# Turning the convolution's result back into rows: 32 by 32 squares on VectorE with a trip through DRAM in place of TensorE transposes

## The chip, the cores and the metric

The kernel runs on one core of a Trainium2 chip. The metric is the device time in microseconds (us) of one execution. Times inside an execution come from one profiled execution, counted from its first instruction. The engines are called PE (TensorE), DVE (VectorE), ACT (ScalarE), POOL (GpSimd) and SP (SyncE, which here only issues DMAs). Weight loads of PE are listed apart as PEld, the issue of a DMA as SPq or ACTq.

## What is computed

One layer on `x` of shape (8, 256, 512): a mixing step and a mixture-of-experts step, each behind a layer norm and with a residual.

```python
x = x + xattn(layernorm(x), k, bias, ctx, ctx, num_heads=8)
x = x + ffn(layernorm(x), gate_w, shared_*, exp_*)

# xattn: D = 256 is split in H = 32 heads of 8 rows, L = 512
kv  = v[:, :, :, None, :] * ctx[:, :, None, :, :]        # 8 x 8 products per head
y   = causal_convolution(kv, k) + kv * bias              # along L, one kernel k per head
out = einsum("bhijl,bhil->bhjl", y, ctx)                 # summed over i
# ffn: shared = silu(x wg) * (x wu) @ wd, plus the top 2 of 8 experts by sigmoid scores
```

The second layer norm needs whole rows: for a row (batch, d), all 512 positions l.

## The kernel before

**Tiles and layouts.** There are 16 tiles of 128 rows (8 batches by 16 values of d); a tile t holds heads 2t and 2t+1. Outside the convolution, a tile is "rows": 128 rows on the partitions, 512 l in each. The convolution wants l on the partitions: four blocks of 128 l, each with 128 rows. Its products with Toeplitz matrices of `k` (L402) run on PE; POOL makes `kv` (`make_kv`, L362); DVE weighs the PSUM result with `ctx` and sums over i into `convT` (`weigh`, L464 and L473), still with l on the partitions. From head 10 on (`H9`) a head takes nine block products in place of ten, with an extra product `same` (L433) and DVE additions (L461).

**Two ways to turn a tile that are there already.** Rows are turned for the convolution and for the shared expert as 32 by 32 squares: ACT writes the normed rows to DRAM (`xv_d` L320, `xn_d` L329), SP reads them back as four quarter loads (`quarters`, L290) so that each 32-row band sits in its place, and one DVE transpose of 128x512 turns all squares (`squares_T`, L296). The last tile, and the first two, go through PE instead: four transposes with the identity into PSUM (L274).

**The result's way back.** `add_skip` (L526) adds the skip term to `convT` of tile t-1 in even head 2t. At the end of that head, behind its convolution products and steps of the shared expert, `residual_T` (L531 to L535) puts four PE transposes into a PSUM tile. In odd head 2t+1, `add_residual` (L538) adds it to the rows of `x2`; bn_stats (L236), ACT's square root, reciprocal and scale follow, then `second_norm` (L326) writes the normed tile to `xn_d`, and SP reads it back as quarters.

**The order of the work is written out by hand.** The loop over 32 heads (L892) emits every engine's instructions in program order, and each engine, and SP's queue, runs its own in that order:

```python
load_toeplitz(h + 2)                 # SP
if not odd: load_tile(t + 3); load_residual(t - 1)   # SP: x1, ctxT, x2
if h == 3: load_shared()             # SP: 4.3 MB of shared weights
...
pss = conv_products(h)               # PE
...                                  # odd: quarters of v, add_residual(t - 1), quarters of f
...                                  # even: add_skip(t - 1), square_vT(t + 1), square_xfT(t - 2)
make_kv(h + 2)                       # POOL
while done < h - 9 + h // (H - 1) and steps[done][0] <= h:
    settle(); step()                 # PE: one step of the shared expert, from head 10 on
if not odd and t > 0:
    residual_T(t - 1)                # PE
```

In heads 0 to 9 the second `weigh` of a head stands behind these DVE operations and the first ahead of them; from head 10 on both stand behind. PSUM for the convolution and the shared expert is one pool of three tiles of two banks (`ps_acc`); an early head takes two of them, so head h+1 needs what `weigh` of head h read first. The transposes' PSUM tiles are the pool `ps_tp` (two tiles). [...] After the heads come the last steps of the shared expert and then the routed experts in blocks of 128 rows, which gather rows from `xn_d` (L1029).

The order of l inside a row (`_orders`, `_laid_out`, L1200 to L1261) is chosen on the host: inputs and weights come permuted, and the result is permuted back.

Of the kernel before, what the change touches and what calls it, by code (L numbers as in the profile page):

```python
# [8 lines left out]
F32 = mybir.dt.float32  # L9
I32 = mybir.dt.int32  # L10
AF = mybir.ActivationFunctionType
ALU = mybir.AluOpType
# [3 lines left out]
P = 128  # L16
B, D, L = 8, 256, 512
NH = 8
H = D // NH
NT = 16  # L20
R = D // NT
NTOK = NT * P
NLB = L // P
# [17 lines left out]
Q = 32  # L41
NQ = P // Q
# [23 lines left out]
def tile_xattn_moe(  # L66
# [29 lines left out]
    V, G, A, T, S = nc.vector, nc.gpsimd, nc.scalar, nc.tensor, nc.sync  # L96
# [3 lines left out]
    def pool(name, bufs=1, stack=ctx, **kw):  # L100
        return stack.enter_context(tc.tile_pool(name=name, bufs=bufs, **kw))
# [4 lines left out]
    dram = pool("dram", space=bass.MemoryType.DRAM)  # L106
    rows = pool("rows", 4)
# [7 lines left out]
    x1, x2, ctxT, tzs = {}, {}, {}, {}  # L115

    def load_tile(t):
        if t < NT:
            x1[t] = cvp.tile([P, L], F32, tag="x1", name=f"x1_{t}")
            S.dma_start(out=x1[t], in_=xv[t])  # L120

            ctxT[t] = cvp.tile([P, NLB + 2, B, R], F32, tag="ctx", name=f"ctxT_{t}", bufs=CTXBUFS)
            S.dma_start(out=ctxT[t], in_=cT[t])
# [6 lines left out]
    def load_toeplitz(h):  # L130

        if h < H:
            tzs[h] = cvp.tile([P, NTZ], F32, tag="tz", name=f"tz_{h}", bufs=TZBUFS)
            S.dma_start(out=tzs[h], in_=toep[h])
# [23 lines left out]
    for e in range(NEXP):  # L158
# [6 lines left out]
        out=upper,  # L165
        in_=upper,
# [30 lines left out]

    xn_d = dram.tile([NTOK + P, L], F32, name="xn_d")
    xv_d = [dram.tile([P, L], F32, name=f"xv_d{t}") for t in range(NT)]
    NCOL = NEXP * CPE  # L200
    table = dram.tile([P * NCOL, 2], F32, name="table")
    zero = rows.tile([P, L], F32, tag="xg", name="zero")
    G.memset(zero, 0.0)
    S.dma_start(out=table.rearrange("(p c) f -> p (c f)", p=P), in_=zero[:, : 2 * NCOL])
    S.dma_start(out=xn_d[NTOK:, :], in_=zero)
# [71 lines left out]
    vT, convT, xfT, xn1, xn2 = {}, {}, {}, {}, {}  # L277
# [31 lines left out]
    def first_root(t):  # L309
        mean, var = ahead[t]  # L310
        ahead[t] = mean, root(f"1_{t}", var, 1.0 / L)
# [213 lines left out]
    def add_skip(t):  # L525
        V.tensor_tensor(convT[t], convT[t], skips.pop(t), ALU.add)  # L526


    res = {}

    def residual_T(t):  # L531
        pt = ps_tp.tile([P, NLB, P], F32, tag="tp", name=f"ptr_{t}")
        for k in range(NLB):
            T.transpose(pt[:, k, :], convT[t][:, k].rearrange("p b r -> p (b r)"), ident)
        res[t] = pt  # L535

    def add_residual(t):
        V.tensor_tensor(x2[t], x2[t], res.pop(t).rearrange("p k l -> p (k l)"), ALU.add)  # L538


    lg, plT, picks = {}, {}, {}
# [91 lines left out]
    def route_places(c):  # L633
# [8 lines left out]
        for n in range(2):  # L642
# [4 lines left out]
            for i in range(TPC):  # L647
# [4 lines left out]
                    in_offset=None,  # L652
                    bounds_check=P * NCOL - 1,
                    oob_is_err=True,
# [98 lines left out]
    for c in range(NCHUNK):  # L753
        steps += [(8 * c + 10, up_step, c, ft) for ft in range(NSF)]

        n = 2 if c < NCHUNK - 2 else 1
# [135 lines left out]
    for h in range(H):  # L892
        t, odd = divmod(h, 2)

        load_toeplitz(h + 2)
        if not odd:
            load_tile(t + 3)
            load_residual(t - 1)
        elif t == NT - 1:
            load_residual(t)  # L900
        if h == 3:
            load_shared()


        if odd and t + 2 < NT:
            first_root(t + 2)
        c, r = divmod(h - 10, 8)
        if c >= 0 and r == 2:
            route_scores(c)
        settle()  # L910
        pss = conv_products(h)
        if h > 1 and not odd:
            skip_turn(t)
        if not odd:
            first_sums(t + 2)
        elif t + 2 < NT:
            first_norm(t + 2)
            quarters(("v", t + 2), xv_d[t + 2])


        nine, picks_here = h >= H9, c >= 0 and r == 2
        if not nine:
            weigh(h, 0, pss[0])
        if odd and t > 0:
            add_residual(t - 1)
            mv = small.tile([P, V.BN_AGGR_DIM], F32, tag="mv", name=f"mv_{h}")
            stats(mv, f"2_{t}", x2[t - 1])
            rt = root(f"2_{t}", mv[:, 1:2], 1.0)
            V.reciprocal(rt, rt)
            nb = small.tile([P, 1], F32, tag="nb", name=f"nb2_{t}", bufs=3)  # L930
            V.tensor_scalar(nb, mv[:, 0:1], rt, -1.0, ALU.mult, ALU.mult)
            second_norm(t - 1, (rt, nb))
            quarters(("f", t - 1), xn_d[(t - 1) * P : t * P, :])
        if not odd and t > 0:
            add_skip(t - 1)
            if t + 1 < NT:
                square_vT(t + 1)
            if t > 1 and not picks_here:
                square_xfT(t - 2)
        if picks_here:  # L940
            route_pick(c)
        if c >= 0 and r == 4:
            route_places(c)
        if nine:
            weigh(h, 1, pss[1])
            weigh(h, 0, pss[0])
            if picks_here:
                square_xfT(t - 2)
        else:
            weigh(h, 1, pss[1])  # L950
        if odd or h == 0:
            skip_sum(t + odd)
        if h == 0:
            skip_turn(0)
        if h == 0:
            make_vT(1)

        if not odd:
            skip_spread(t)
        make_kv(h + 2)  # L960
        if not odd:
            skip_products(t + 1)

        while done < h - 9 + h // (H - 1) and steps[done][0] <= h:
            settle()
            step()

        if not odd and t > 0:
            residual_T(t - 1)
        if c >= 0:  # L970
            if r == 0:
                route_logits(c)
            if r == 1:
                route_T(c)
            if r == 3:
                route_ranks(c)


    last_t, last_c = NT - 1, NCHUNK - 1
# [3 lines left out]
    step()  # L983
    residual_T(last_t)
    settle()
    add_residual(last_t)
    mv = small.tile([P, V.BN_AGGR_DIM], F32, tag="mv", name="mv_last")
    stats(mv, "2_last", x2[last_t])
    second_norm(last_t, rstd_of(mv, "_last"))
# [80 lines left out]
    for e in range(NEXP):  # L1070
        wde = wd_sb[:, e].rearrange("p (t d) -> p t d", d=L)
        S.dma_start(
            out=wde[:, 0:2, :], in_=ed[e, 0 : 2 * P].rearrange("(t p) d -> p t d", p=P)
# [126 lines left out]
def _orders():  # L1200

    import numpy as np

    l = np.arange(L).reshape(NLB, 2, HP)
    ins = [l[mb, ::-1] if SIN[mb] else l[mb] for mb in BIN]
    outs = [l[lb, ::-1] if SOUT[lb] else l[lb] for lb in BOUT]
    return [np.concatenate(o).reshape(L) for o in (ins, outs)]


def _laid_out(a):  # L1210

    import numpy as np

    def by_quarter(w):

        return w.reshape(NQ, NLB, Q, -1).transpose(1, 0, 2, 3).reshape(L, -1)


    _, outs = _orders()
    a = {n: v[..., outs] if v.shape[-1] == L and n != "L0_xattn_k" else v for n, v in a.items()}  # L1220
    a["L0_ffn_shared_wd"], a["L0_ffn_exp_wd"] = (
        a["L0_ffn_shared_wd"][outs],
        a["L0_ffn_exp_wd"][:, outs],
    )

    ins = np.argsort(outs)[_orders()[0]]
    lag = np.arange(HP)[None, :] - np.arange(HP)[:, None]
    padded = np.concatenate([np.zeros((H, P), np.float32), a["L0_xattn_k"]], axis=1)
    toep = np.concatenate(
        [  # L1230
            np.concatenate([padded[:, P + d * HP + lag] for d in above_below], axis=1)
            for above_below in TZ
        ],
        axis=2,
    )
    x = a["x"].reshape(B, NT, R, L).transpose(1, 0, 2, 3).reshape(NT, P, L)
    c = a["ctx_2048"].reshape(B, NT, R, L)
    c = np.concatenate([c[..., ins], c[..., 2 * P :]], axis=-1).reshape(B, NT, R, NLB + 2, P)

    g, u = a["L0_ffn_shared_wg"].T, a["L0_ffn_shared_wu"].T  # L1240
    cols = [w[:, f : f + P] for f in range(0, SFF, P) for w in (g, u)]
    sgu = np.concatenate(cols, axis=1)
    sgu = by_quarter(sgu).reshape(NLB, P, 2 * SFF).transpose(1, 0, 2)
    gu = np.stack([a["L0_ffn_exp_wg"], a["L0_ffn_exp_wu"]], axis=1)

    gu = gu.reshape(NEXP, 2, FF, NQ, NLB, Q).transpose(0, 3, 5, 1, 4, 2)
    nf = len(F_TILES)
    squares = [q * nf + t for t in range(nf) for q in range(NQ) if q * nf + t < FF // Q]
    order = [s * Q + a for s in squares for a in range(Q)]
    return {  # L1250
        "x": x,
        "xv": x[..., ins],
        "cT": c.transpose(1, 4, 3, 0, 2),
        "toep": toep,
        "skip": a["fside_S2_0"],
        "gwT": by_quarter(a["L0_ffn_gate_w"].T),
        "sgu": sgu,
        "sd": a["L0_ffn_shared_wd"].T,
        "egu": gu.reshape(NEXP, P, NGU),
        "ed": a["L0_ffn_exp_wd"].transpose(0, 2, 1)[:, order],  # L1260
    }  # L1261
# [24 lines left out]
```

## Time and profile before

| | |
|---|---|
| three timed runs | 794.74, 799.49, 799.99 us; median 799.49 us |
| profiled execution | 795.8 us, span 794.1 us from first to last instruction |
| mean granted clock of TensorE | 0.989 |
| PE matmul groups, busy | convolution L402 192.0 us for one form and 47.2 for another, shared expert L674 155.0 and L718 70.2, routed experts L1088 176.1 and L1146 98.6 |
| PE transposes of the result, L534 | 64 in 16 groups of four, 9.8 us busy |
| DVE | 535.3 us busy; weighing L464 and L473 78.1 us each, squares L296 29 of about 0.70 us |
| DMA | 89.10 MB, mean 112 GB/s |

The page lists busy times of each engine, forty slices of the span, DMA queues, the chain that ended last, the costliest groups of instructions, and DMA issues with the time to landing. The trace behind it can be asked for one engine's instructions in order of time (start, duration, engine, line, operation, tiles, count; in square brackets how long the engine was idle before and what ended that), for who waited for whom, and for busy times by stage. Matmuls are pipelined, so a busy PE is not a PE at its peak, and the distance between starts says more than durations do.

### The profile page before, as it was taken

To read this page: it belongs to the slowest core of one execution; us is meant where nothing else is said; L and a number is where in the kernel's file an instruction comes from. 1 tells how busy PE (TensorE), PEld (TensorE's weight loads), DVE (VectorE), ACT (ScalarE), POOL (GpSimd) and SP (SyncE) were. 2 spreads that over 40 slices of the span, in tenths; PEclk is the share of its full clock that TensorE was granted. 3 is DMA by queue.
4 is the path that set the end of the run, shared out by engine and by line. 5 is a ranking of instruction groups with operands and counts; after the bars stand their busy time and mean duration, and the time that the engine had idled before them with its cause. 6 is when DMAs were issued, how large, how long until landed. Compare 5 with 4: busy or idle time off the path is not lost. (4 is left out here: it accounts for less than half of the span.)

```text
span 794.1 us, 8485 instructions
## 1 busy us (share of the span) xinstructions
PE 767.9 (97%) x2379; PEld 353.8 (45%) x2379; DVE 535.3 (67%) x1209; ACT 203.1 (26%) x381; POOL 472.6 (60%) x474
## 2 busy tenths in 40 slices
PE   7999999999999999999999999999999999999991
PEld 4333333443333443433443444455555555555550
DVE  2768867768557768557766263288877877887750
ACT  2222254344144335135313210011111111111110
POOL 7767793469372559462640042766778777777421
PEclk9999999999999999999999999999999999999996
DMA  6495434234413234312100690395443444344332
GB/s 232 121 323 205 152 113 139 88 53 140 144 48 120 77 83 140 112 48 87 46 27 27 279 369 23 105 282 116 76 74 68 76 75 74 68 77 73 61 40 27
DMA packets 52142, 89.10 MB, mean 112 GB/s; under 512 B 8832, under 2 KB 24064, under 8 KB 50944
## 3 DMA queue, kind: packets, MB, share of 16 engines
q1 hardware_dynamic: 36960, 61.77, 24.1%
q0 software_dynamic: 10816, 18.92, 13.9%
q10 hardware_dynamic: 4320, 7.87, 2.7%
q8 instruction: 21, 0.34, 0.2%
q14 instruction: 25, 0.20, 0.1%
HBM read 66.34 MB, written 22.18 MB: 111 GB/s over the span
## 5 line engine op out<-in xcount | busy, mean ns | idle before, releaser
L402 PE MATMUL cv<-kv,tz 128*64 128x512 f32 (+2 forms) x720 | 192.0, 609 | 1.8 <-POOL kv L362 1.8
L1029 POOL DMA_INDIRECT xg<-xn_d,src x144 | 146.8, 1020 | 56.6 <-issue 39.1
L1088 PE MATMUL up<-wgu_sb,xT 128*128 (+1 forms) x576 | 176.1, 459 | 1.4 <-DVE x L743 1.4
L674 PE MATMUL gu<-xfT,wsh 128*128 128x512 f32 x352 | 155.0, 593 | 1.6 <-issue 1.6
L1132 DVE STREAM_TRANSPOSE hTb<-h 32x96 f32<-32x96 f32 (+1 forms) x560 | 146.3, 261 | 8.2
L362 POOL TENSOR_TENSOR kv<-vT,ctxT 128x512 f32<-128x512 f32 x128 | 132.5, 1067 | 15.0 <-PE cv L402 4.8
L1088 PEld LDWEIGHTS up<-wgu_sb,xT 128*128 128x128 f32 x576 | 109.2, 190 | 72.0 <-issue 15.6
L402 PEld LDWEIGHTS cv<-kv,tz 128*64 128x64 f32 (+2 forms) x720 | 61.4, 150 | 122.3 <-issue 98.5
L674 PEld LDWEIGHTS gu<-xfT,wsh 128*128 128x128 f32 x352 | 66.5, 190 | 85.0 <-issue 83.8
L1146 PE MATMUL y<-wd_sb,hTb 128*128 (+3 forms) x216 | 98.6, 593 | 0.8 <-ACT hTb L1121 0.8
L464 DVE TENSOR_TENSOR prod<-cv,ctxT 128x1024 f32<-128x1024 f32 x64 | 78.1, 1221 | 17.6 <-PE cv L402 15.9
L648 POOL DMA_INDIRECT table<-entries,to x32 | 31.8, 994 | 90.4 <-DVE at L644 81.9
L1155 POOL DMA_INDIRECT out_dram<-ys,row x36 | 58.2, 1616 | 45.0 <-ACT ys L1154 21.3
L473 DVE TENSOR_REDUCE convT<-prod 128x128 f32<-128x1024 f32 x64 | 78.1, 1220 | 2.2
L718 PE MATMUL dn<-wshd,hT 128*128 128x512 f32 x160 | 70.2, 593 | 0.0
L1146 PEld LDWEIGHTS y<-wd_sb,hTb 128*128 128x128 f32 (+1 forms) x216 | 41.0, 190 | 43.1 <-issue 34.7
L1096 ACT ACTIVATE h<-up 128x352 f32<-128x352 f32 x36 | 16.7, 464 | 165.6 <-PE up L1088 165.6
L518 POOL TENSOR_TENSOR skip<-ctxT,w 128x512 f32<-128x512 f32 x16 | 17.7, 1106 | 65.7 <-ACT w L510 36.5
L688 ACT ACTIVATE sg<-gu 128x512 f32<-128x512 f32 (+1 forms) x24 | 14.3, 596 | 164.6 <-PE gu L674 164.6
L1097 DVE TENSOR_TENSOR h<-h,up 128x352 f32<-128x352 f32 x36 | 18.6, 517 | 42.8 <-ACT h L1096 42.8
L402 PE MATMUL cv<-kv,td 128*128 128x512 f32 x88 | 47.2, 618 | 0.0
L718 PEld LDWEIGHTS dn<-wshd,hT 128*128 128x128 f32 x160 | 30.2, 190 | 37.6 <-issue 37.6
(145 smaller groups left out, 603.4 us busy)
## 6 DMA issues: line engine op xcount, KB each, us to landing
tz<-in_toep_dram SPq DMA_DIRECT2D x32, 384.0 KB, 3.4
wgu_sb<-in_egu_dram SPq DMA_DIRECT2D x8, 1408.0 KB, 16.3
ctxT<-in_cT_dram SPq DMA_DIRECT2D x16, 384.0 KB, 4.7
x<-in_xv_dram SPq DMA_DIRECT2D x16, 256.0 KB, 3.6
x<-in_x_dram SPq DMA_DIRECT2D x16, 256.0 KB, 4.8
xn_d<-xn ACTq DMA_DIRECT2D x16, 256.0 KB, 2.4
out_dram<-x SPq DMA_DIRECT2D x16, 256.0 KB, 2.4
wd_sb<-in_ed_dram SPq DMA_DIRECT2D x8, 512.0 KB, 10.8
```

Source lines behind the costliest of these rows:

```text
L362: G.tensor_tensor(kv[:, mb], vT[t][:, at, :, cols].unsqueeze(2).to_broadcast([P, B, NH, NH]), ctxT[t][:, at, :, cols].unsqueeze(3).to_broa ...
L402: T.matmul(banks[lb][cols], lhsT=w, rhs=x, start=first, stop=left[lb][here[0]] == 0,)
L464: V.tensor_tensor(prod, ps.rearrange("p k b j i -> p (k b) j i"), ctxT[t][:, 2 + 2 * n : 4 + 2 * n, :, cols] .rearrange("p k b i -> p (k b ...
L473: V.tensor_reduce(convT[t][:, two, :, cols].rearrange("p k b j -> p (k b) j"), prod, AX.X, ALU.add)
L648: ins = G.indirect_dma_start(out=table, out_offset=bass.IndirectOffsetOnAxis(ap=to[:, i : i + 1], axis=0), in_=entry[:, i, n, :], in_offse ...
L674: T.matmul(ps, lhsT=wsh[:, k, m0 : m0 + m], rhs=rhs[k], start=(k == 0), stop=(k == NLB - 1))
L718: T.matmul(ps, lhsT=hTs[c][:, ft, i * P : (i + 1) * P], rhs=wshd[:, ft, :], start=(ft == 0), stop=False,)
L1029: G.indirect_dma_start(out=xgs[k][:, c, :], out_offset=None, in_=xn_q, in_offset=bass.IndirectOffsetOnAxis(ap=src[:, c, k : k + 1], axis=0 ...
L1088: T.matmul(ps[:, m, :FF], lhsT=xTs[k][:, j].rearrange("p c b -> p (c b)"), rhs=wk[:, bass.ds(eks[k] * NGU + (m * NLB + j) * FF, FF)], star ...
L1132: V.transpose(hT[q * Q : (q + 1) * Q, :n, c], hk[c * Q : (c + 1) * Q, q * NF * Q : (q * NF + n) * Q].rearrange("p (t a) -> p t a", a=Q),)
L1146: T.matmul(ps, lhsT=hT[:fw, ft].rearrange("p c b -> p (c b)"), rhs=wk[:fw, bass.ds(eks[k] * NWD + ft * L, L)], start=(ft == 0), stop=(ft = ...
L1155: G.indirect_dma_start(out=out, out_offset=bass.IndirectOffsetOnAxis(ap=row[:, k : k + 1], axis=0), in_=y, in_offset=None, bounds_check=NT ...
```

## The change

For tiles 0 to 14 the four PE transposes at the end of the even head are gone. In their place, right behind `add_skip`, DVE transposes all 32 by 32 squares of `convT` into `rt` (128x512), SP stores `rt` to DRAM (256 KB), and SP loads it back with four loads of 64 KB into `rd`, each setting one band of 32 rows in place. `add_residual` reads `rd` from SBUF. `rt` and `rd` take turns in a tag of three buffers that the routed experts use later. The last tile keeps PE's transposes, with an addition in another order of elements. The squares leave l in another order within a row than before; `_orders` gives this third order, and the inputs, weights and the result's permutation on the host follow it.

```diff
+    cv_d = [dram.tile([P, L], F32, name=f"cv_d{t}") for t in range(NT - 1)]
...
+    def residual_squares(t):
+
+        rt = rows.tile([P, NQ, NLB, Q], F32, tag="xT", name=f"rt_{t}", bufs=3)
+        V.transpose(
+            rt,
+            convT[t].rearrange("p k b r -> p k (b r)").rearrange("p k (j b) -> p j k b", b=Q),
+        )
+        S.dma_start(out=cv_d[t], in_=rt.rearrange("p j k a -> p (j k a)"))
+        rd = rows.tile([P, NQ, NLB, Q], F32, tag="xT", name=f"rd_{t}", bufs=3)
+        for j in range(NQ):
+            S.dma_start(
+                out=rd[j * Q : (j + 1) * Q].rearrange("p i k a -> p i (k a)"),
+                in_=cv_d[t][:, j * P : (j + 1) * P].rearrange("(i b) m -> b i m", b=Q),
+            )
+        res[t] = rd.rearrange("p i k a -> p (i k a)")
+
     def add_residual(t):
-        V.tensor_tensor(x2[t], x2[t], res.pop(t).rearrange("p k l -> p (k l)"), ALU.add)
+        V.tensor_tensor(x2[t], x2[t], res.pop(t), ALU.add)
+
+    def add_last_residual(t):
+        ps = res.pop(t).rearrange("p k (i a) -> p k i a", a=Q)
+        v = x2[t].rearrange("p (i k a) -> p k i a", i=NQ, a=Q)
+        V.tensor_tensor(v, v, ps, ALU.add)
...
         if not odd and t > 0:
             add_skip(t - 1)
+            residual_squares(t - 1)
             if t + 1 < NT:
                 square_vT(t + 1)
...
-        if not odd and t > 0:
-            residual_T(t - 1)
         if c >= 0:
...
     residual_T(last_t)
     settle()
-    add_residual(last_t)
+    add_last_residual(last_t)
...
-    return [np.concatenate(o).reshape(L) for o in (ins, outs)]
+    ins, outs = [np.concatenate(o).reshape(L) for o in (ins, outs)]
+
+    return ins, outs, outs.reshape(NLB, NQ, Q).transpose(1, 0, 2).reshape(L)
...
-    ins = np.argsort(outs)[_orders()[0]]
+    ins, outs = np.argsort(rows)[ins], np.argsort(rows)[outs]
...
-    c = np.concatenate([c[..., ins], c[..., 2 * P :]], axis=-1).reshape(B, NT, R, NLB + 2, P)
+    c = np.concatenate([c[..., ins], c[..., outs[2 * P :]]], axis=-1).reshape(B, NT, R, NLB + 2, P)
```

More of the change, by code (lines that the diff above doesn't have):

```diff
@@ L1216, in by_quarter @@
         return w.reshape(NQ, NLB, Q, -1).transpose(1, 0, 2, 3).reshape(L, -1)
-    _, outs = _orders()
-    a = {n: v[..., outs] if v.shape[-1] == L and n != "L0_xattn_k" else v for n, v in a.items()}
+    ins, outs, rows = _orders()
+    a = {n: v[..., rows] if v.shape[-1] == L and n != "L0_xattn_k" else v for n, v in a.items()}
     a["L0_ffn_shared_wd"], a["L0_ffn_exp_wd"] = (
-        a["L0_ffn_shared_wd"][outs],
-        a["L0_ffn_exp_wd"][:, outs],
+        a["L0_ffn_shared_wd"][rows],
+        a["L0_ffn_exp_wd"][:, rows],
     )
-    ins = np.argsort(outs)[_orders()[0]]
+    ins, outs = np.argsort(rows)[ins], np.argsort(rows)[outs]
     lag = np.arange(HP)[None, :] - np.arange(HP)[:, None]
@@ L1283 @@
     r = _run(nc, [arrays], core_ids=[0])
-    o = r.results[0]["out_0_dram"][:NTOK, _np.argsort(_orders()[1])].reshape(NT, B, R, L)
+    o = r.results[0]["out_0_dram"][:NTOK, _np.argsort(_orders()[2])].reshape(NT, B, R, L)
     return _np.ascontiguousarray(o.transpose(1, 0, 2, 3)).reshape(B, D, L)
```

## The prediction

> **What bounds the kernel now.** I read the busy times, then the stages, then the neighbourhood of the operations that change.
>
> ```profile
> PE 767.9 (97%) x2379; PEld 353.8 (45%) x2379; DVE 535.3 (67%) x1209; ACT 203.1 (26%) x381; POOL 472.6 (60%) x474
> ```
> ```profile
> 60.00:90.00 30.00, 29.85 (x104) 11.04 (x104) 26.45 (x36) 9.37 (x24) 20.72 (x20) 1.00 0.53 182
> ...
> 150.00:180.00 30.00, 30.00 (x102) 12.61 (x98) 20.34 (x33) 11.84 (x22) 15.01 (x15) 1.00 0.38 92
> ```
>
> The first line is of the page, the others of the stages: after the window come its length and the busy us of PE, PEld, DVE, ACT, POOL, then clock, DMA share and GB/s. PE is the bound throughout. But the spare time differs: in heads 2 to 9 (about 30 to 97 us) VectorE is busy 26.45 of 30 us, from head 10 (97 to 440 us) only about 20. So the change meets two regimes.
>
> The transposes' true price is a start-to-start distance, since matmuls overlap. From PE's timeline:
>
> ```profile
> 88.63 0.60 PE L534 MATMUL ptr<-ident,convT 128*128 128x128 f32 x4
> 89.16 8.30 PE L402 MATMUL cv<-kv,tz 128*64 128x512 f32 x28
> ...
> 385.96 0.60 PE L534 MATMUL ptr<-ident,convT 128*128 128x128 f32 x4
> 386.40 1.02 PE L433 MATMUL same<-ks,tz 128*128 128x512 f32 x2
> ```
>
> What follows starts 0.53 and 0.44 us after the first transpose. That, not 4 x 0.27 us, is what four transposes take from the bound.
>
> The early heads on VectorE, then on SP's queue, then the times to landing (last column, us):
>
> ```profile
> 63.25 0.68 DVE L538 TENSOR_TENSOR x<-x,ptr 128x512 f32<-128x512 f32 x1
> ...
> 72.21 0.71 DVE L296 STREAM_TRANSPOSE xfT<-xq_f 128x512 f32<-128x512 f32 x1
> ...
> 77.16 1.22 DVE L464 TENSOR_TENSOR prod<-cv,ctxT 128x1024 f32<-128x1024 f32 x1 [1.81 <-PE cv L402]
> ...
> 79.55 0.68 DVE L538 TENSOR_TENSOR x<-x,ptr 128x512 f32<-128x512 f32 x1
> ```
> ```profile
> 68.79 1.73 SPq L290 DMA_DIRECT2D xq_f<-xn_d  x4
> 70.62 0.38 SPq L134 DMA_DIRECT2D tz<-in_toep_dram  x1
> 71.09 0.38 SPq L120 DMA_DIRECT2D x<-in_xv_dram  x1
> 71.52 0.42 SPq L123 DMA_DIRECT2D ctxT<-in_cT_dram  x1
> 71.99 0.42 SPq L128 DMA_DIRECT2D x<-in_x_dram  x1
> 72.54 0.35 SPq L134 DMA_DIRECT2D tz<-in_toep_dram  x1
> ```
> ```profile
> x<-in_x_dram SPq DMA_DIRECT2D x16, 256.0 KB, 4.8
> ...
> wshd<-in_sd_dram SPq DMA_DIRECT2D x1, 1280.0 KB, 14.2
> ```
>
> The residual adds come every 16.6 us ((96.46 - 63.25) / 2; the third is at 96.46), and VectorE's waits for PE in such a period are only about 2 us (1.81 at 77.16; 0.46 + 1.76 in the next). SP works in bursts, and the last load of a burst needs 5 us to land because the others lie ahead of it.
>
> [...] the x2 load at 71.99 lands after 5.0 us, a 64 KB xq_f load with nothing ahead after 2.0. [...] Here the clock stayed at 1.00 across PE's longest wait once the heads run, 1.58 us at 106.41; a longer one is not shown.
>
> **Part by part.** *PE, removed:* 15 of 16 groups of four transposes. Heads 2, 4, 6, 8: 0.53 + 0.54 + 0.58 + 0.53 = 2.2, and 0.3 us of waiting for the skip sum at 71.67: 2.5. Heads 10 to 30, the eleven distances to the next start (0.43 to 0.53): 5.2. Together -7.7 us at most.
>
> *DVE, added:* 15 transposes of 128x512 at 0.70 us (the vT row's mean, same size) = 10.5 us. In heads 10 to 30 VectorE has about 10 spare us in 30. In a full one of them, head 28, its last PSUM read ends at 383.7 (382.46 + 1.22), and head 29, whose products take that buffer again, starts at 386.40. So 0.7 us are covered: 0. With the cover gone it would be 11 x 0.7 = 7.7, and the weighing of PSUM would be what comes late. In heads 2 to 8 the spare 1.8 us of a period covers it alone, not together with a wait. The last tile's add reads and writes in runs of 32, same element count, about 0.68 us: 0. The new order of l is done on the host; instruction sizes stay: 0.
>
> *SP, added:* per tile one 256 KB store and four 64 KB loads, placed in the even head behind that head's burst (tz, x1, ctxT, x2). The four loads wait for the store. Moved behind them: the odd head's tz load, and the quarter loads after it. From head 10 on this is free: after the burst at 155.46 to 157.26 SP waits, the next burst lies some 30 us off, and the add comes about 14 us after the skip sum (373.44 to 388.12 in heads 28 and 29), against 0.7 + some 4 + 3.4 us for transpose, store and loads: 0. If that cover went, each head's add would hold VectorE's whole row of PSUM reads.
>
> In heads 2 to 9 it is not free; two costs.
>
> *First, once:* the Toeplitz load at 37.72 and the shared weights at 38.09 are issued in head 3, now behind tile 0's loads: rt done 38.0, store lands 40.1, four loads to 41.6, so the weights go out from about 42.5, 4.4 us late. wshd then lands near 57.5 instead of 53; head 4's xq_v, queued behind it, held VectorE at 55.47 already (1.2 us) and now comes near 59.5; xq_f near 60.5. Then tile 1's burst, store (66.0) and loads (69.4): residual add 1 at about 69.5 instead of 63.25: +6.2. On the way VectorE runs both squares (to 61.7), head 4's second weighing (2.4), a reciprocal and head 5's first product, whose PSUM read ends near 65.4; head 6, which needs that buffer, could start at 62.1 (63.2 now, less two groups of transposes): PE waits 3.3 us.
>
> *Second, a ring of waits.* From one residual add to the next: add to xn_d's issue 3.28 (63.25 to 66.53); landing 2.2; xq_f's first issue to x2's issue 3.25 (68.79 to 71.99 and SP's step); x2 lands 5.0; the store behind it 0.65 more (an estimate, 256 KB at the 400 GB/s at which 2816 KB of wsh passed in about 7 us); four loads 0.05 + 1.35 + 2.0 = 3.4. Sum 17.8 us, above the 16.6 of now and 16.1 without transposes. Bounds: 15.0 if the store did not queue (the 5.65 become SP's 0.5 and xn_d's 2.4), which binds nothing; 18.8 if the loads take 3.0 us, the median of xq_v between 30 and 75 us. I take 17.8. Two turns, add 1 to add 3: 2 x 1.2 = +2.4.
>
> So add 3 moves from 96.46 to about 105.1 (+8.6). From it hangs, already today, the first shared product: 96.46, xn_d, xq_f, square at 105.60 (2.48 us waited for the DMA), PE at 106.41 (1.58 us waited). That distance of 9.95 stays: PE gets there at 115.0, +8.6, in which the -2.5 of the early transposes is swallowed. After it only the -5.2 counts.
>
> Sum: +8.6 - 5.2 = +3.4 us. The profiled execution took 795.8 us (span 794.1): 799.2. The three timed runs have a median of 799.49, 3.7 above it; the same addition there gives 802.9. I forecast 802.
>
> **Rivals.**
> *A, above (chance 0.50):* 802, own range 797 to 807. For it: bursts and landings in order. Against: the estimates for store and weights add up over four tiles.
> *B, only the displaced weights cost (0.15):* the ring stays below 16.6. Head 6 loses some 3.3 us and nothing follows: -7.7 + 3.3 = -4.4, 795.
> *C, the round trip is hidden (0.19):* -7.7, so 791.8. For it: the xq loads with the same round trip cost the kernel only 5.2 us of DVE waits. Against: they have a whole head and no burst ahead of them.
> *D, slower (0.16):* PE's new waits halve its clock. In A, walking the heads as above, they are about 3.3, 2.0, 1.6, 3.2 and 2.3 us (heads 6, 7, 9, the diagonal products of 10, the first shared product)[...]. [...] 808 to 811. Against: none yet at 1.58 us.
> The change cannot fail to do what it says: the instruction order on PE has no ptr group but the last tile's.
>
> **How the numbers follow.** About 1% is what a measurement of this kernel can tell from no change: 8 us, below 791.5 or above 807.5. C at 791.8 lies on the lower bound: half of it (0.09) plus a little of B's spread (0.02) is faster, 0.11. Slower: D (0.16) and a little of A's tail (0.03), 0.19. Within: 0.70. The range holds A, B, half of C and most of D: 791 to 810.
>
> **What would show it.** No L534 but one group. The new transposes near 0.70 us. SP's timeline: store about 0.5 us after each x2 load in heads 4 to 8, landing 5 us later, wsh issued near 42.5. DVE: waits for rd at L554 in heads 5, 7, 9 of about 2.4 us, adds near 69.5, 87, 105, and none from head 11 on. PE: first shared product near 115, and from there everything 0.44 to 0.53 us per tile earlier. A first shared product before 107 would refute ring and weights; clock slices under 1.00 after 60 us would speak for D.

## The result and the profile after

The changed kernel took 808.41 us (median of four runs, 807.03 to 809.32) against 797.77 us for the kernel before on the same chip (794.74 to 799.99): ratio 1.0124, 95% interval [1.009, 1.0157], so 7.2 to 12.5 us slower. The profiled execution's span went from 794.1 to 805.3 us (+11.2); the forecast's sum was +3.4. Up to L196 lines of the kernel after are those of before, then one later; behind the new functions some 22 later.

The page's busy times, then the stages (columns as in the prediction), after and before:

```profile
PE 769.1 (95%) x2319; PEld 348.4 (43%) x2319; DVE 556.7 (69%) x1224; ACT 203.1 (25%) x381; POOL 477.8 (59%) x474
```
```profile
60.00:97.00 37.00, 32.16 (x94) 10.45 (x94) 27.93 (x36) 8.26 (x21) 24.32 (x22) 0.95 0.59 174
97.00:445.00 348.00, 340.29 (x1038) 131.55 (x1036) 260.43 (x394) 129.97 (x238) 200.20 (x190) 1.00 0.37 110
```
```profile
60.00:97.00 37.00, 36.85 (x128) 13.71 (x127) 31.63 (x41) 10.47 (x26) 27.64 (x27) 1.00 0.53 184
97.00:445.00 348.00, 345.77 (x1091) 138.21 (x1090) 237.03 (x380) 130.06 (x236) 188.40 (x182) 1.00 0.29 88
```

PE's busy time has not fallen by the 9.8 us of its transposes; its share of the span fell. Between 60 and 97 us PE stands still for 4.84 us in 37 (0.15 before), and VectorE does less, not more (27.93 against 31.63): both wait. From 97 us on VectorE is 23.4 us busier. Twelve transposes of 0.70 us are 8.4 of it, and some 4 are work that the delay carried into this stretch, less what it carried out of it; about 11 are left. That number is the thread to a cause that the prediction did not see. PE's clock shows 0.95 in the first row.

Four rows of the waits of after (us in total, times, longest):

```profile
PE cv L403 <- DVE prod L465: 11.2, 7, 2.9
PEld cv L403 <- DVE prod L465: 9.0, 3, 3.8
DVE x L555 <- DMA rd<-cv_d: 9.5, 3, 3.6
DVE vT L297 <- DMA xq_v<-xv_d: 5.5, 1, 5.5
```

Three adds waited for the trip through DRAM, and no more than three. One transpose waited 5.5 us for a load that the weights had been put ahead of. PE waited for VectorE's products. VectorE's timeline places the waits:

```profile
60.19 0.71 DVE L297 STREAM_TRANSPOSE vT<-xq_v 128x512 f32<-128x512 f32 x1 [5.51 <-DMA xq_v<-xv_d]
...
70.25 1.12 DVE L555 TENSOR_TENSOR x<-x,rd 128x512 f32<-128x512 f32 x1 [3.23 <-DMA rd<-cv_d]
...
89.93 0.93 DVE L555 TENSOR_TENSOR x<-x,rd 128x512 f32<-128x512 f32 x1 [3.59 <-DMA rd<-cv_d]
...
108.12 1.04 DVE L555 TENSOR_TENSOR x<-x,rd 128x512 f32<-128x512 f32 x1 [2.71 <-DMA rd<-cv_d]
```

All four waits lie in heads 4 to 9. The first shared product, before and after:

```profile
106.41 7.11 PE L674 MATMUL gu<-xfT,wsh 128*128 128x512 f32 x16 [1.58 <-issue]
```
```profile
118.00 7.10 PE L696 MATMUL gu<-xfT,wsh 128*128 128x512 f32 x16 [0.25 <-issue]
```

Aligned at the same instruction, PE in after is late by: 11.59 us here; from here 0.43 to 0.49 us less at each removed group, 4.7 in all (net of two steps of 0.1 the other way); but 2.6 us more within head 16 and 2.35 us more within head 24; 11.8 us at the end of the heads, 11.7 in the routed experts, and 11.2 at the last store of the span. So +11.6 - 4.7 + 4.9 = +11.8 at the end of the heads, and behind them the delay shrinks by 0.6. The early stretch is what the prediction had at +8.6. The 4.9 us in heads 16 and 24 are in no step of it. This is the first of the two, on VectorE, then on GpSimd, then on PE:

```profile
187.31 4.88 DVE L555 TENSOR_TENSOR x<-x,rd 128x512 f32<-128x512 f32 x1
...
194.55 1.23 DVE L465 TENSOR_TENSOR prod<-cv,ctxT 128x1024 f32<-128x1024 f32 x1
...
197.67 1.22 DVE L465 TENSOR_TENSOR prod<-cv,ctxT 128x1024 f32<-128x1024 f32 x1
```
```profile
186.26 4.13 POOL L363 TENSOR_TENSOR kv<-vT,ctxT 128x512 f32<-128x512 f32 x4
190.35 1.26 POOL L373 TENSOR_TENSOR ks<-kv 128x512 f32<-128x512 f32 x1
191.58 1.19 POOL L377 TENSOR_TENSOR td<-tz 128x256 f32<-128x256 f32 x1
```
```profile
196.06 1.10 PE L434 MATMUL same<-ks,tz 128*128 128x512 f32 x2 [0.43 <-DVE prod L465]
198.95 1.98 PE L403 MATMUL cv<-kv,tz 128*128 128x512 f32 x4 [1.79 <-DVE prod L465]
```

The add took 4.88 us in place of 0.69. It began as a row of GpSimd operations ran, ended 0.58 us after `ks` (191.61), and the last of the row, `td`, took 1.19 us in place of 0.72: the add was held until `ks` was done, and then held `td`. In the kernel before the same add ran over the same GpSimd row in 0.69 us, and PE took head 16's products from VectorE with nothing to spare (VectorE first, then GpSimd, then PE):

```profile
176.47 0.69 DVE L538 TENSOR_TENSOR x<-x,ptr 128x512 f32<-128x512 f32 x1
...
184.79 1.22 DVE L464 TENSOR_TENSOR prod<-cv,ctxT 128x1024 f32<-128x1024 f32 x1
```
```profile
174.80 4.13 POOL L362 TENSOR_TENSOR kv<-vT,ctxT 128x512 f32<-128x512 f32 x4
178.90 1.26 POOL L372 TENSOR_TENSOR ks<-kv 128x512 f32<-128x512 f32 x1
180.13 0.72 POOL L376 TENSOR_TENSOR td<-tz 128x256 f32<-128x256 f32 x1
```
```profile
185.20 1.02 PE L433 MATMUL same<-ks,tz 128*128 128x512 f32 x2
186.07 1.98 PE L402 MATMUL cv<-kv,tz 128*128 128x512 f32 x4
```

The product's read of PSUM ends at 184.79 + 1.22 = 186.01, PE needs that buffer at 186.07. What differs is the add's second input: in PSUM before (`ptr`), in SBUF after (`rd`). The fifteen adds of after take 0.69 to 1.28 us, and 4.88 and 4.63 in heads 15 and 23; those of before take 0.67 to 0.69. From 97 us on that is about 11 us more, the 11 that were left.

The short adds above 0.69 us follow GpSimd to the hundredth: those at 157.70 and 250.53 met a GpSimd instruction that had 0.25 and 0.46 us to run, and took 0.80 and 1.01, each 0.55 more than that, and `ks` behind the first of them, at 157.91, took 1.72 in place of 1.26. The long ones go further: behind the last 0.01 us of one `kv`, the add at 187.31 lost not one turn but four in a row, to three more `kv` (1.02 to 1.03 us from start to start) and to `ks`.

### The profile page after: what moved, and what is told of

Same layout as the page of the kernel before. It is cut to its first block, busy times and chain, and to the rows that moved or that the text cites. A ratio compares the mean times of both kernels' runs of the same rounds, so it can differ in the third digit from the quotient of the medians.

```text
span 805.3 us, 8497 instructions
## 1 busy us (share of the span) xinstructions
PE 769.1 (95%) x2319; PEld 348.4 (43%) x2319; DVE 556.7 (69%) x1224; ACT 203.1 (25%) x381; POOL 477.8 (59%) x474
## 5 line engine op out<-in xcount | busy, mean ns | idle before, releaser
L403 PE MATMUL cv<-kv,tz 128*64 128x512 f32 (+2 forms) x720 | 198.4, 619 | 13.2 <-DVE prod L465 11.2
L363 POOL TENSOR_TENSOR kv<-vT,ctxT 128x512 f32<-128x512 f32 x128 | 134.2, 1080 | 22.3 <-issue 14.7
```

The costliest lines, as they stand in the source:

```text
L363: G.tensor_tensor(kv[:, mb], vT[t][:, at, :, cols].unsqueeze(2).to_broadcast([P, B, NH, NH]), ctxT[t][:, at, :, cols].unsqueeze(3).to_broa ...
L403: T.matmul(banks[lb][cols], lhsT=w, rhs=x, start=first, stop=left[lb][here[0]] == 0,)
```

## The experiments

Theory T1: the loss lies in heads 2 to 9, as a ring of waits through SP's queue (add, normed store, quarter loads, burst, residual store, residual loads, add) together with the displaced weights. Theory T2: 4.9 us are the add's two SBUF inputs meeting GpSimd in heads 15 and 23, where PE's buffers have no slack. Rivals: the added VectorE work itself; the traffic of 7.9 MB more; PE's clock, halved by its waits. The first 30 us of a profiled execution, ahead of everything that the change touches, took up to 1.9 us more or less than in the kernel before; where it matters this shift is named, and "net" means less it. It goes with the time that the granted clock stood at half between 8 and 16 us: 3.41 us in the kernels before and after, 6.83 in `early_pe` (late by 1.85), `tile0_pe`, `trip_unread` and `before_dve`, none in `late_pe` (early by 1.4). A wait further on can swallow a shift, so net figures are good to about 1.5 us.

**1 and 2: one half of the tiles each.** In `early_pe` tiles 0 to 3 keep PE's transposes and the rest take squares; in `late_pe` it is the reverse.

```diff
+FIRST_SQ = 4
-            residual_squares(t - 1)
+            if t - 1 >= FIRST_SQ: residual_squares(t - 1)     # late_pe: <
...
+        if not odd and 0 < t <= FIRST_SQ: residual_T(t - 1)   # late_pe: t > FIRST_SQ
```

> Tiles 0 to 3 (heads 2 to 9) go back to rows by TensorE, tiles 4 to 14 by squares and DRAM. Theory (a ring of waits through SP's bursts in the early heads, and in the later heads a residual add that is held up by GpSimd because both its inputs are now in SBUF): the first shared product comes within 0.5 us of the kernel before (106.4), the eleven removed groups give 5.2 us, the two long adds in heads 15 and 23 take about 4.9 us back: span 793 to 795. Rival 1 (the loss is VectorE's added transposes, even over the tiles): about 11/15 of the 11.2 us remain, span 802. Rival 2 (only the ring costs, the long adds are hidden elsewhere): span 789.

> The complement: tiles 0 to 3 by squares and DRAM, tiles 4 to 14 by TensorE. Theory: the first shared product comes near 118.0 as in the changed kernel (11.6 us late) and nothing is gained or lost after it: span 805.5 to 806. Rival 1 (loss even over the tiles): span about 797.

`early_pe`: 798.57 against 798.83, ratio 1.0003 [0.9982, 1.0024]. Its first shared product stands where the shift puts it (+1.85 us), no add waits; but adds of 4.90 us (at 177.57) and 4.65 (at 299.51) are there, and in each of heads 16 and 24 PE has 2.41 us from its second `same` product to the next start (0.44 in the kernel before). Its span, 798.1, lies above the 793 to 795 expected: 1.85 us is the shift, and a stretch at half speed at 490 us added 1.7. `late_pe`: 1.0153 [1.0115, 1.0191]; its first shared product is 11.44 us late, and it stays 11.4 to 11.8 late from there. So the whole net loss sits in heads 2 to 9, and eleven squares in the later heads gain nothing: what the groups give back, the two long adds take.

**3 and 4: the add's input moved, badly.** `psum_add` has ScalarE copy `rd` into PSUM immediately ahead of the add; `before_sbuf_add` has the kernel before copy PSUM into SBUF there.

```diff
 def add_residual(t):                                   # psum_add
+    pr = ps_tp.tile([P, L], F32, tag="tp", name=f"pr_{t}")
+    A.copy(pr, res.pop(t))
-    V.tensor_tensor(x2[t], x2[t], res.pop(t), ALU.add)
+    V.tensor_tensor(x2[t], x2[t], pr, ALU.add)
```

> The changed kernel, but ScalarE copies the loaded rows into PSUM and the residual add reads them there, so that it has one SBUF input as before. Theory: every residual add takes about 0.68 us again, PE's two waits of 2.4 us in heads 16 and 24 vanish, the early heads keep their ring: span 799.5 to 801. Rival (VectorE's extra 0.7 us per tile makes heads 15 and 23 late): the two waits stay, span about 805.

> The kernel before, but ScalarE copies the transposed result from PSUM into SBUF, and the residual add reads it there. No DRAM trip, no squares on VectorE. Theory (two SBUF inputs): adds of 4 to 5 us in heads 15 and 23, two PE waits of about 2.4 us after them, the other adds 0.8 to 1.2 us: span about 799. Rival: the add is as short as from PSUM, span 794.

`psum_add`: 1.0146 [1.0102, 1.019]. Every add takes 0.69 us, as T2 says, but the copies queue behind ScalarE's other work, most adds wait 3.5 to 4.1 us for them, and PE's 2.41 us stay. Its span, 804.8, is what the rival had (about 805). `before_sbuf_add`: 1.009 [1.0058, 1.0122]; its adds, too, waited for ScalarE (up to 3.92 us), and those of heads 15 and 23 took 2.44 and 2.18 us, not the 4 to 5 expected. In both, the edit added a wait of the size in question, so neither decides between T2 and the rival. The copy had to go where ScalarE has time.

**5: the copy made early.** `early_pe_psum2` is `early_pe` with the copy at the end of the even head, half a tile ahead of the add.

```diff
+        if not odd and t > FIRST_SQ:
+            residual_to_psum(t - 1)      # A.copy(pr, rd); the add reads pr
```

> Tiles 0 to 3 by TensorE; tiles 4 to 14 by squares and DRAM, with a ScalarE copy of the loaded rows into PSUM late in the even head, long before the add, so that the add has one SBUF input and comes no later. Theory (the long adds of heads 15 and 23 are two SBUF inputs behind GpSimd's instructions): all adds 0.7 us, PE's two waits of 2.4 us in heads 16 and 24 are gone, the distance from the first shared product to the routed experts is 5 us shorter than before, ratio about 0.994. Rival (VectorE's added 0.7 us makes those heads late): the waits stay at 2 us or more, ratio 1.000.

791.5 against 796.15: ratio 0.9927 [0.991, 0.9943], faster than both kernels. The add and the product behind it in head 15, and PE:

```profile
178.25 0.67 DVE L561 TENSOR_TENSOR x<-x,pr 128x512 f32<-128x512 f32 x1
...
186.13 1.23 DVE L466 TENSOR_TENSOR prod<-cv,ctxT 128x1024 f32<-128x1024 f32 x1
```
```profile
186.54 1.02 PE L435 MATMUL same<-ks,tz 128*128 128x512 f32 x2
187.41 1.98 PE L404 MATMUL cv<-kv,tz 128*128 128x512 f32 x4
```

PE goes from `same` to the next product in 0.87 us, without a wait, as in the kernel before; all these adds take 0.67 to 0.68 us. Against `early_pe` only the place of one input is changed, at the price of eleven ScalarE copies of 0.59 us.

**6: the reverse, in the kernel before.** `before_sbuf_add2` has no squares, no trip, no new DMA: ScalarE copies the transposes' result from PSUM to SBUF behind the next tile's root, and the add reads it there.

```diff
         if odd and t + 2 < NT: first_root(t + 2)
+        if odd and t > 0: residual_to_sbuf(t - 1)   # A.copy(rd, ptr)
```

> The kernel before with its transposed result copied by ScalarE into SBUF right behind the next tile's square root, which VectorE waits for just ahead of the add anyway; the add then reads two SBUF tiles. No DRAM trip, no squares added on VectorE. Theory (two SBUF inputs behind GpSimd): adds of 0.8 to 1.3 us in most later heads and of more than 4 us in heads 15 and 23, PE waits there of about 2.5 us each, span about 799. Rival: every add about 0.7 us, span 794 to 795.

1.0059 [1.0036, 1.0082]. In head 15, VectorE, GpSimd, PE:

```profile
176.15 3.91 DVE L543 TENSOR_TENSOR x<-x,rd 128x512 f32<-128x512 f32 x1 [0.31 <-ACT rd L539]
```
```profile
177.19 1.05 POOL L362 TENSOR_TENSOR kv<-vT,ctxT 128x512 f32<-128x512 f32 x1
178.22 1.27 POOL L372 TENSOR_TENSOR ks<-kv 128x512 f32<-128x512 f32 x1
179.45 1.19 POOL L376 TENSOR_TENSOR td<-tz 128x256 f32<-128x256 f32 x1
```
```profile
186.82 1.98 PE L402 MATMUL cv<-kv,tz 128*128 128x512 f32 x4 [1.31 <-DVE prod L464]
```

The add ends 0.57 us after `ks` (179.49), and `td` takes 1.19 us again. In head 23 the add takes 5.55 us; PE loses 1.5 us in head 16 and 3.1 in head 24 (about 2.5 each expected). Experiments 5 and 6 together show T2: with the input in PSUM the long adds and PE's waits go, with it in SBUF they come, with or without the trip. That GpSimd's instructions are what holds the add is read from the times, but without an exception: all 75 residual adds of these runs that read two SBUF inputs and took over 0.7 us end 0.54 to 0.60 us behind the end of a GpSimd instruction.

**7: the burst's order.** `burst_last` puts the loads of x1 and ctxT behind the residual's (x2 stays ahead).

```diff
-        load_tile(t + 3)                  # head of the even head
...
             residual_squares(t - 1)
+            load_tile(t + 3)
```

> The changed kernel with the loads of x1 and ctxT moved behind the residual's store and loads in SP's order (the x2 load stays ahead). Theory (ring of waits): the store then has only tz and x2 ahead of it, a turn of the ring is about 15.6 us and binds no longer; what stays is the later shared weights (add 1 some 3 to 5 us late) and the two waits in heads 16 and 24. First shared product near 110 in place of 118, span 796 to 799. Rival (the early loss is the shared weights alone): first shared product still near 117, span 804.

1.0122 [1.0102, 1.0143]. The ring's turns are 18.5 and 15.5 us (19.68 and 18.19 in after), the last add waits for nothing, and the first shared product is 8.30 us late in place of 11.59. I had expected about 110 us there; it is 114.7. So the order on the queue is worth 3.3 us, not all of the ring. In this run PE then ran at half speed for a while at that product and in heads 16 and 24 (mean granted clock 0.980, 0.985 in after), which cost some 1.6 us each and ate the gain: the span was 806.4, where 796 to 799 had been expected.

**8: the weights' place.** `tile0_pe` is the changed kernel with `FIRST_SQ = 1`: tile 0 alone by PE, so that the shared weights go out early as before.

> The changed kernel with tile 0 alone by TensorE, so that the shared weights are issued as early as before (38.1). Theory: residual add 1 comes near 63.5 instead of 70.2, the ring then still turns twice at 18 to 19.7 us: add 3 near 100.5 to 102 and the first shared product near 111 (118 in the changed kernel, 106.4 before). Rival 1 (weights alone): the first shared product at 106 to 107. Rival 2 (ring alone): at 117 or later.

One run, 807.14 us, span 805.4. Add 1 came at 68.86, 4.1 us late net of a shift of 1.5, where I had expected none: it waited 3.87 us for `rd`, so the trip holds tile 1's add without any weights in the way. The first shared product, at 116.33, is 8.4 us late net: 114.8, where I had expected 111.

**9: the trip without its reader.** In `trip_unread` every tile goes by PE; tiles 0 to 3 also make squares, store and loads, which nothing reads.

```diff
-        res[t] = rd.rearrange("p i k a -> p (i k a)")     # nothing reads rd
...
+            residual_T(t - 1)                             # for every tile
```

> All tiles go back to rows by TensorE, and the residual adds read PSUM. For tiles 0 to 3 VectorE's squares, the store and the four loads are made as well, in the changed kernel's places, but nothing reads them. Theory (a ring closed by the add's wait for the loads): the ring is open, so only the later shared weights and SP's delays remain: first shared product 3 to 5 us later than before (109.5 to 111.5). Rival (the added DMAs and VectorE's added work in themselves): near 117.

One run, 800.01 us. No add waits; they follow each other after 16.33 and 16.88 us. The wait behind the weights is there:

```profile
61.76 0.71 DVE L298 STREAM_TRANSPOSE vT<-xq_v 128x512 f32<-128x512 f32 x1 [5.10 <-DMA xq_v<-xv_d]
...
68.46 0.68 DVE L560 TENSOR_TENSOR x<-x,ptr 128x512 f32<-128x512 f32 x1
...
84.79 0.68 DVE L560 TENSOR_TENSOR x<-x,ptr 128x512 f32<-128x512 f32 x1
...
101.67 0.68 DVE L560 TENSOR_TENSOR x<-x,ptr 128x512 f32<-128x512 f32 x1
```

The first shared product is about 3.7 us late net, with all of PE's groups in place. So the traffic and the displaced weights cost 3.7 us, and the rest needs the add's wait. The parts fit roughly: the 3.7 of this run and the 8.4 of `tile0_pe`, whose ring has no displaced weights, make 12.1, where after is 11.6 late. Each is one run, each carries a part of the added traffic, and net figures are good to about 1.5 us, so the shares are rough; that the larger one is the ring's stands.

**10: VectorE's new work alone.** `before_dve` is the kernel before with fifteen squares more on VectorE, in the same place, which nothing reads.

> The kernel before with the 15 squares added on VectorE behind each skip sum, their result unread: no DMA, no change of the add. Theory: VectorE's added 10.5 us are covered; first shared product within 1 us of before, no waits of 2 us in heads 16 and 24, span 794 to 796. Rival (VectorE's load is what costs): span above 799.

0.9996 [0.9984, 1.0008]; behind a shift of 1.6 us nothing is lost anywhere. The 10.5 us of transposes are covered: VectorE's added work in itself is not the cause.

**11 and 12: everything mended, all tiles by squares.** `all_fixed` takes the PSUM copy from tile 4 on, x1 and ctxT behind the residual's loads, and the weights in pieces at the ends of heads 2, 4, 6 and 8. `all_fixed2` differs in the weights alone.

```diff
-        for n in {2: (0,), 4: (1,), 6: (2,), 8: (3, NLB)}.get(h, ()): load_shared(n)
+        if h == 2:                    # ahead of tile 0's squares
+            for n in range(NLB): load_shared(n)
...
+        if h == 12: load_shared(NLB)  # wshd
```

> The changed kernel, all 15 tiles by squares and DRAM, with three mends: the shared weights in five pieces at the ends of heads 2 to 8, x1 and ctxT behind the residual's loads, and from tile 4 on the early ScalarE copy into PSUM. Theory: no displaced weights, the ring at 15.6 to 18.5 us a turn, no long adds later: first shared product at 107 to 111, span 788 to 793, ratio near that of the version with tiles 0 to 3 by TensorE. Rival (the early heads lose by something else): first shared product above 114, span 796 or more.

> The changed kernel with every suspected cost of the early heads and of the adds taken away at once, and with all fifteen tiles still turned by squares: the shared expert's first weights (2.8 MB) go out at the start of head 2, where SP's queue waited some 6 us for the first tile's squares, the rest (1.3 MB) only at the end of head 12; the loads of x1 and ctxT stand behind the residual's four loads; from tile 4 on ScalarE copies the residual into PSUM late in the even head, so the add has one SBUF input. My theory (ring of waits and displaced weights in heads 2 to 9, two SBUF inputs in heads 15 and 23): the first shared product comes 2 to 5 us after that of the kernel before, not 11.6; nothing is lost in heads 16 and 24; the removed groups give back 5 us after it; the profiled span ends between 788 and 795, a ratio of 0.990 to 0.999. If the weights in the previous attempt were not what held the first shared product (PE reaches it at 114 or later again), the ring itself does not yield to order on SP's queue, and the time stays at 800 or above. A clock at half speed behind one of PE's remaining waits in heads 6 to 10 would show as 1 to 2 us more at the first shared product.

`all_fixed`: 1.0074 [1.0053, 1.0095]. Head 10 begins only 2.9 us late, but the last pieces, issued at 100 to 102.7 and landed at 112.1, lie ahead of head 10's loads:

```profile
117.22 9.05 PE L703 MATMUL gu<-xfT,wsh 128*128 128x512 f32 x14 [7.74 <-DVE xfT L299]
```

Of the 10.8 us lost there (107 to 111 expected, 117.2 measured), 4.6 were lost before, at the diagonal products at 105.46; the rest came from where I put the weights. `all_fixed2`: 794.88 against 795.56, ratio 0.9986 [0.9963, 1.001], no difference; the kernel with all tiles turned by squares has caught up, but no more. Its first shared product is 7.28 us late (2 to 5 expected), and from there it gains 4.7 us to the end of the heads (2.56 late) and loses nothing in heads 16 and 24. The ring has not gone:

```profile
49.17 1.37 DVE L562 TENSOR_TENSOR x<-x,rd 128x512 f32<-128x512 f32 x1 [3.87 <-DMA rd<-cv_d]
...
66.85 1.14 DVE L562 TENSOR_TENSOR x<-x,rd 128x512 f32<-128x512 f32 x1 [1.74 <-DMA rd<-cv_d]
...
84.52 0.92 DVE L562 TENSOR_TENSOR x<-x,rd 128x512 f32<-128x512 f32 x1 [1.10 <-DMA rd<-cv_d]
...
103.54 1.25 DVE L562 TENSOR_TENSOR x<-x,rd 128x512 f32<-128x512 f32 x1 [2.75 <-DMA rd<-cv_d]
```

Its turns are 17.68, 17.67 and 19.02 us. The store still lands 3.6 to 4.3 us after its issue, with the loads of tz and x2 ahead of it, and in the last turn the loads that were moved behind the residual lie ahead of the normed tile's store, which lands in 3.64 us in place of 2.00. Whether taking tz and x2 from SP's queue as well would open the ring was not tried.

## Why the prediction was right in kind and too low in size

**The end.** The median, 808.4, lies inside the range of 791 to 810 and above the own range of the likeliest case (797 to 807). Part of that is luck: the range went up to 810 to make room for D, a cause that cost nothing here, and a cost that the prediction had not counted filled this room. The mechanism forecast, ring and displaced weights, is shown by experiments 1, 2, 8 and 9; the early sizes (3.0 us too low), a missing step (4.9) and the groups' gain (0.5 too high) make up the 7.8 us between +3.4 and +11.2, less the 0.6 by which the delay shrinks at the end.

**First, once (weights).** As forecast: wsh went out at 42.56 (42.5 forecast), xq_v held VectorE until 60.19 (59.5). Residual add 1 came at 70.25, forecast 69.5: 0.75 more.

**Second, the ring of waits.** This is the mis-sized term. Forecast 17.8 us per turn, measured 19.68 and 18.19:

| from, to | forecast | first turn | second turn |
|---|---|---|---|
| add to the first xq_f load's issue | 5.5 | 5.79 | 5.58 |
| to x2's issue | 3.25 | 4.15 | 3.20 |
| to the store's landing | 5.65 | 5.37 | 5.83 |
| to the next add | 3.4 | 4.37 | 3.58 |

The residual loads did wait for their stores (SP 41.0 us in 15 waits, up to 5.1). The store's landing, which held the only estimate in the sum, was right to 0.3 us; the sum was low because the other legs were read from one undisturbed instance each: x1's issue took SP 1.05 us in place of 0.38, the last residual load landed in 2.74 us in place of 2.0, and the add itself takes 0.9 to 1.1 us with its new input. SP's timeline of the first turn:

```profile
78.61 1.05 SPq L120 DMA_DIRECT2D x<-in_xv_dram  x1
79.75 0.38 SPq L123 DMA_DIRECT2D ctxT<-in_cT_dram  x1
80.19 0.43 SPq L128 DMA_DIRECT2D x<-in_x_dram  x1
80.70 0.39 SPq L545 DMA_DIRECT2D cv_d<-rt  x1
85.62 1.78 SPq L548 DMA_DIRECT2D rd<-cv_d  x4
```

Add 3 at 108.12 is 3.0 us above the forecast 105.1 (0.75 + 1.9 + 0.4); the distance from it to the first shared product, 9.88, is the forecast 9.95. So 118.0 in place of 115.0, and the chain held link by link.

**PE, removed.** 5.2 us after head 10 forecast; 4.7 by the balance above, and in `all_fixed2`, where the heads from 10 on lose nothing else, 7.28 - 2.56 = 4.7. A removed group brought the next start forward by 0.43 to 0.49 us, also where the distance read ahead was 0.53. The 2.5 of the early groups were swallowed, as forecast.

**DVE, added.** "So 0.7 us are covered: 0" is right (`before_dve`). But the section costed only the new instructions. That the fifteen adds change an input from PSUM to SBUF stands in no step: this is where the prediction failed, by 4.9 us. And its test of the cover took "a full one ... head 28", where the shortest should have been taken: heads 15 and 23, with eight shared products ahead of the next head (3.60 us), in which VectorE had 0.06 us to spare.

**SP in heads from 10 on: 0.** Right: no add from head 11 on waits for `rd`.

**The rivals.** B and C fell with the adds' waits at 70.25, 89.93 and 108.12. D's sign, a clock under 1.00 after 60 us, is there, but not its price. Its size, 808 to 811, was my estimate: in the kernel before the granted clock is 1.00 from 12.82 to 780.82 us, so nothing there shows what a wait of PE costs in clock. In after PE did run at half speed behind waits, twice, for 3.41 us each, from 77.93 us behind a wait of 1.98 us and from 112.06 behind one of 2.94:

```profile
112.07 4.63 PE L403 MATMUL cv<-kv,tz 128*64 128x512 f32 x16 [2.94 <-DVE prod L465]
```

The same sixteen took 2.96 us in `all_fixed2`, at 107.70, behind a longer wait (3.98). In after this cost nothing, since the first shared product behind it waited for `xfT` (until 117.9); the other slow stretch, to 81.34, lies in the ring, where PE waits as well. That the time came out where D had put it, 808 to 811, is no support for it.

## What to carry to other kernels

When a result takes a new path, write down for each reader not only when the operand comes but where it comes from: an add whose second input moves from PSUM to SBUF is another instruction, and its price depends on what GpSimd does at that moment (0.67 to 0.69 us from PSUM in before, 0.69 to 4.88 from SBUF in after). Test a cover at the stage with the least slack (here the short heads), not at a typical one. A ring of waits through one queue, as SP's here, is the sum of its legs, and legs taken from their best instances make a sum that no turn reaches (17.8 us forecast, 19.68 and 18.19 measured); such a trip belongs where the ring has slack, which here is from the fifth tile on (0.9927 with the copy into PSUM, 1.0003 without it), and not ahead of it.

## What the runs showed of the hardware that I had not expected

- A VectorE add of two SBUF inputs (128x512) that meets GpSimd work mostly takes what is left of GpSimd's instruction and 0.55 us, 0.71 to 1.78 us in all in these runs; GpSimd's next instruction is then held in turn (in after `ks` took 1.72 us in place of 1.26, `td` 1.19 in place of 0.72). But in heads 15 and 23 it took 2.18 to 5.55 us: it lost one to four further turns, mostly up to the end of `ks`, in one case (5.55 us) two operations beyond it. What decides between the two these runs leave open.
- PE's clock halved behind waits of 1.98 and 2.94 us in after (0.51 in the mean from 77.9 to 81.4 us and from 112.0 to 115.5) and of 1.84 us in all in head 24 of `burst_last`, but not behind one of 3.98 us in `all_fixed2` (sixteen products in 2.96 us behind it, 4.63 behind the 2.94 in after). In after half speed lasted 3.41 us each time. So the length of a wait alone does not decide; what else does these runs leave open.
- A 256 KB store with nothing ahead landed in 2.0 us (in after at 144.0), behind 256 and 384 KB loads of the same queue in 4.8 to 5.6 in after (at 61.1, 80.7, 99.3 and 117.5) and in 3.6 to 4.3 in `all_fixed2`.
